# The last sequence's FC chunks led by four steps, and its last two chunks projected tile by tile

## The chip, the cores and the metric

The kernel runs on one core of one Trainium2 chip. The metric is the device time of one execution in microseconds; of several executions the median is taken. Beside the times there is one execution that the hardware profiler recorded; views of its trace are called "the profile" here. The engines of a core are TensorE (PE, its weight loads PEld), VectorE (DVE), ScalarE (ACT), GpSimd (POOL) and SyncE (SP), which issues the DMAs.

## The reference

The input is a batch of 8 sequences of 512 tokens by 512 features. A first stage adds to x a four-layer bidirectional gated recurrence (a linear scan) of the normalised x, fused by a matrix. The second stage, which the change is in, is a feed-forward block with ternary weights:

```python
h = jnp.einsum('btd,hd->bth', x, absmean(W_fc))       # 512 -> 2048
h = jax.nn.gelu(h, approximate=False)
h = layernorm(h, ln_w, ln_b)                          # over the 2048
return jnp.einsum('bth,dh->btd', h, absmean(W_proj))  # 2048 -> 512
```

Its input is the normalised result of the first stage, and its output is added to that result. absmean makes weights of -1, 0 and 1.

## The kernel before, in words

The recurrent stage takes lines 207 to 731 and leaves its result in DRAM. The feed-forward stage begins at line 739. Its order of work is written out by hand: the program issues instructions in the order of the code, and each engine runs its own in that order.

Names: B = 8 sequences, NF = 16 chunks of 128 hidden features, NT = 4 tiles of 128 tokens, NC_ = 4 chunks of 128 input features, LAG = 2.

- `fc(b, k)` (L777) computes chunk k of sequence b for all 512 tokens: eight matmuls (L782, four input chunks, each as a high and a low part) into one of two PSUM banks `ph`. ScalarE makes `g` (Gelu, L786), `sq` (L788) and `ghi` (L790, g times the norm's weight, rounded). VectorE adds g and sq to the running sums `acc` (L797), and makes the low part `glo` (L799).
- `proj(b, k, ghi, glo)` (L804) adds the chunk's share to the output: for each of the four token tiles two matmuls (L809) into that tile's own bank `po`, so eight matmuls. The four banks hold all 16 chunks' sums of a sequence.
- `token_stats(b)` (L814) makes the layer norm's mean and factor of each token from the two sums, which is possible only when all 16 chunks are in them: eight transposes on TensorE (L820), two reductions on VectorE (L821), small VectorE operations (L822 to L826), a power on GpSimd (L828). Its second half `last` (L830) makes `nmr` on VectorE (L832) and, for the last sequence only, the four centerings (L842) of the output rows.
- `finish(b)` (L849) empties the banks. For the last sequence VectorE does it, bank times the token's factor plus the row (L855), and `store` (L846) issues the tile's store on SP's queue. For the others ScalarE copies the banks (L859), and VectorE's centering and the store follow in later steps, one tile each, from the list `rests`.

The loop (L880) has a step j for each chunk of all sequences, and LAG more. In a step come, on TensorE: fc of chunk j, in the first step of a sequence the transposes of the statistics of the sequence before, and the projection of the chunk of two steps before. `waiting` holds the chunks between the two. Behind it come the second halves in `late`. The last sequence's chunks are j = 112 to 127. Steps 128 and 129 have no fc left: step 128 has the statistics' transposes, then the projection of chunk 126, then the rest of the statistics and the centerings; step 129 has the projection of chunk 127 and `finish`.

`gpool` holds g and sq three deep, `partp` holds ghi and glo four deep.

Of the kernel before, what the change touches and what calls it, by code (L numbers as in the profile page):

```python
# [9 lines left out]
F32 = mybir.dt.float32  # L10
F32R = mybir.dt.float32r
AF = mybir.ActivationFunctionType
ALU = mybir.AluOpType
# [3 lines left out]
P = 128  # L17
# [7 lines left out]
def kernel(  # L25
# [26 lines left out]
    nc = tc.nc  # L52
    B, S, H = x.shape
# [3 lines left out]
    NT = S // P  # L57
    NF = F // P
# [11 lines left out]
    tokp = ctx.enter_context(tc.tile_pool(name="tok", bufs=TOK))  # L70
# [21 lines left out]
    xs = {}  # L92
# [70 lines left out]
    def normalise(dst, src, rs_nmu, name):  # L163
        rs, nmu = rs_nmu
        nmr = small.tile([P, 1], F32, tag="nmr", name=f"nmr_{name}")
        nc.scalar.activation(nmr, nmu, AF.Copy, scale=rs)  # L166
        nc.scalar.activation(dst, src, AF.Identity, bias=nmr, scale=rs)  # L167
# [13 lines left out]
    def load_y(b):  # L181

        for t in range(NT):
            xs["y", b, t] = xsp.tile([P, H], F32, tag="xs", name=f"xy_{b}_{t}")
            nc.sync.dma_start(out=xs["y", b, t], in_=x1[b][t])
# [18 lines left out]
    rows = {}  # L204


    with rec:
# [129 lines left out]
        rx, scale = {}, {}  # L337
# [398 lines left out]

    gpool = ctx.enter_context(tc.tile_pool(name="g", bufs=3, reuse_waits="tile"))
    partp = ctx.enter_context(tc.tile_pool(name="parts", bufs=4, reuse_waits="tile"))  # L740
    accp = ctx.enter_context(tc.tile_pool(name="acc", bufs=1, reuse_waits="tile"))
    ps_x = ctx.enter_context(tc.tile_pool(name="ps_x", bufs=2, space=PSUM, reuse_waits="tile"))
    ps_o = ctx.enter_context(tc.tile_pool(name="ps_o", bufs=1, space=PSUM, reuse_waits="tile"))
    LAG = 2
# [30 lines left out]
    acc, po, first, stat = {}, {}, {}, {}  # L775

    def fc(b, k):  # L777
        ph = ps_f.tile([P, S], F32, tag="pf", name=f"ph_{b}_{k}")
        for c in range(NC_):
            w = fcq[k // NP_][:, c, ts(k % NP_, P)]  # L780
            for i in range(2):
                nc.tensor.matmul(  # L782
                    ph, lhsT=w, rhs=ys[b][c][i], start=(c == 0 and i == 0), stop=(c == NC_ - 1 and i == 1),
                )
        g = gpool.tile([P, S], F32, tag="g", name=f"g_{b}_{k}")
        nc.scalar.activation(g, ph, AF.Gelu)  # L786
        sq = gpool.tile([P, S], F32, tag="sq", name=f"sq_{b}_{k}")
        nc.scalar.activation(sq, g, AF.Square)  # L788
        ghi = partp.tile([P, S], F32R, tag="ghi", name=f"ghi_{b}_{k}")
        nc.scalar.activation(ghi, g, AF.Copy, scale=lnw[:, k : k + 1])  # L790
        if k == 0:
            first[b] = (g, sq)
        else:
            if k == 1:
                acc[b] = [accp.tile([P, S], F32, tag=f"acc{i}", name=f"acc{i}_{b}") for i in range(2)]
            for i, v in enumerate((g, sq)):
                nc.vector.tensor_tensor(acc[b][i], first[b][i] if k == 1 else acc[b][i], v, ALU.add)  # L797
        glo = partp.tile([P, S], F32R, tag="glo", name=f"glo_{b}_{k}")
        nc.vector.scalar_tensor_tensor(  # L799
            glo, g, lnw[:, k : k + 1], ghi.bitcast(F32), ALU.mult, ALU.subtract  # L800
        )
        return ghi, glo

    def proj(b, k, *parts):  # L804
        if k == 0:
            po[b] = [ps_o.tile([P, H], F32, tag=f"po{t}", name=f"po_{b}_{t}") for t in range(NT)]
        for t in range(NT):
            for i, part in enumerate(parts):
                nc.tensor.matmul(  # L809
                    po[b][t], lhsT=part[:, ts(t, P)], rhs=pwq[k // NP_][:, k % NP_, :],  # L810
                    start=(k == 0 and i == 0), stop=(k == NF - 1 and i == 1),
                )

    def token_stats(b):  # L814

        su = small.tile([P, 2, NT], F32, tag="su", name=f"su_{b}")
        for i, v in enumerate(acc.pop(b)):
            pst = ps_x.tile([P, 512], F32, tag="px", name=f"pst_{b}_{i}")
            for t in range(NT):
                nc.tensor.transpose(pst[:, ts(t, P)], v[:, ts(t, P)], ident)  # L820
            nc.vector.tensor_reduce(su[:, i, :], pst.rearrange("p (t f) -> p t f", t=NT), AX.X, ALU.add)  # L821
        nc.vector.tensor_scalar(su, su, 1.0 / F, None, ALU.mult)  # L822
        var = small.tile([P, NT], F32, tag="var", name=f"var_{b}")
        nc.vector.tensor_tensor(var, su[:, 0, :], su[:, 0, :], ALU.mult)
        nc.vector.tensor_tensor(var, su[:, 1, :], var, ALU.subtract)
        nc.vector.tensor_scalar(var, var, 0.0, LN_EPS, ALU.max, ALU.add)  # L826
        rs = small.tile([P, NT], F32, tag="rsg", name=f"rsg_{b}")
        nc.gpsimd.tensor_tensor(rs, var, mhalf.broadcast_to([P, NT]), ALU.pow)  # L828

        def last():  # L830
            nmr = small.tile([P, NT], F32, tag="nmrg", name=f"nmrg_{b}")
            nc.vector.scalar_tensor_tensor(nmr, su[:, 0, :], -1.0, rs, ALU.mult, ALU.mult)  # L832
            stat[b] = (rs, nmr)
            if b == B - 1:
                for t in range(NT):
                    center(b, t, xs["y", b, t])
        return last

    def center(b, t, rows_in):

        xt = xs["y", b, t]
        nc.vector.scalar_tensor_tensor(rows_in, rows[0], stat[b][1][:, t : t + 1], rows_in, ALU.mult, ALU.add)  # L842
        if rows_in is not xt:
            nc.vector.tensor_tensor(xt, xt, rows_in, ALU.add)

    def store(b, t):  # L846
        nc.sync.dma_start(out=out[b, ts(t, P), :], in_=xs["y", b, t])

    def finish(b):  # L849

        for t in range(NT):
            rs = stat[b][0][:, t : t + 1]
            if b == B - 1:
                row = xs["y", b, t]
                nc.vector.scalar_tensor_tensor(row, po[b][t], rs, row, ALU.mult, ALU.add)  # L855
                store(b, t)
            else:
                scaled = tokp.tile([P, H], F32, tag="tok", name=f"scaled_{b}_{t}")
                nc.scalar.activation(scaled, po[b][t], AF.Copy, scale=rs)  # L859

                def rest(t=t, scaled=scaled):
                    center(b, t, scaled)
                    store(b, t)
                rests.append(rest)

    rests = []
    found, ytok = {}, {}

    def y_stats(b, ts_):
        for t in ts_:  # L870
            found[t] = stats(xs["y", b, t], f"y{b}_{t}")

    def y_tokens(b, ts_):
        for t in ts_:
            tok = tokp.tile([P, H], F32, tag="tok", name=f"ytok_{b}_{t}")
            normalise(tok, xs["y", b, t], found.pop(t), f"y{b}_{t}")
            ytok.setdefault(b, []).append(tok)

    waiting = []
    for j in range(B * NF + LAG):  # L880
        b, k = divmod(j, NF)
        late = []
        if b < B:
            waiting.append((b, k, *fc(b, k)))
        if k == 0 and b > 0:
            late.append(token_stats(b - 1))
        if b == 0 and 5 <= k < 5 + NC_ + 3:
            row_piece(k - 5)
        if b + 1 < B and k >= NF - NC_:
            px = ps_x.tile([P, S], F32, tag="px", name=f"py_{b + 1}_{k}")  # L890
            late.append(y_chunk(b + 1, ytok[b + 1], k - (NF - NC_), px))
        if j >= LAG:
            done = waiting.pop(0)
            proj(*done)
        for f in late:
            f()
        if rests:
            rests.pop(0)()
        if j >= LAG and done[1] == NF - 1:
            finish(done[0])  # L900
        if b < B:
            at = 12 if b == 0 else 8
            if at <= k < at + NT:
                xt = xs["y", b, k - at]
                nc.vector.tensor_tensor(xt, xt, rows[1], ALU.add)
            if b + 1 < B:
                if k == 2:
                    load_y(b + 1)
                if k in (6, 7):
                    y_stats(b + 1, (2 * k - 12, 2 * k - 11))  # L910
                if k in (8, 9):
                    y_tokens(b + 1, (2 * k - 16, 2 * k - 15))


# [41 lines left out]
```

## Time and profile before

| | |
|---|---|
| median of 3 runs | 1767.56 us (1766.42 to 1767.7) |
| the profiled execution, its own time | 1769.31 us |
| its span, first to last instruction | 1767.3 us |
| mean granted TensorE clock | 0.990 |
| FC matmuls of the feed-forward stage (L782) | 1024 of 390 ns |
| projection matmuls (L809) | 512 of 398 ns, 512 of 390 ns |
| Gelu (L786) | 128 of 597 ns, idle before them 245.9 us, ended by PE ph |
| stores of the output | 32 of 256 KB, 2.0 us to landing |

A line of the timeline gives start, duration, engine, source line, operation, what it writes and reads, its shape and count, and in brackets the idle time before it and who ended it. A matmul's duration is longer than its distance to the next, since matmuls overlap; where a stage is bound by TensorE, the distance of the starts counts. Where several instructions are merged (x2, x4), the duration is from the first start to the last end.

### The profile page before, as it was taken

Reading aid. Unit: us, or ns where it says so; the run is one execution under the profiler, and the core shown is the slowest. Engines: PE = TensorE matmul, PEld = TensorE weight load, DVE = VectorE, ACT = ScalarE, POOL = GpSimd, SP = SyncE. Lnnn points to the kernel's source line nnn. Section 1 sums busy time; section 2 is a strip of 40 time slices with the busy share of each in tenths; the row PEclk is TensorE's granted clock in tenths of the full one; section 3 lists DMA queues with packets and bytes.
Section 4 is the critical chain, followed back from the end, with each engine's and each line's share of the span. In section 5 each row is a group of like instructions: output and inputs, shape, how many; then the busy total and the mean of one; then the engine's idle time right before and its main releaser. Section 6 shows DMA issues by size and latency. Waiting matters only on the chain.

```text
span 1767.3 us, 19729 instructions
## 1 busy us (share of the span) xinstructions
PE 1721.4 (97%) x6424; PEld 1046.7 (59%) x6424; DVE 1451.1 (82%) x2865; ACT 1066.2 (60%) x1836; POOL 214.5 (12%) x334
## 2 busy tenths in 40 slices
PE   7989999999999999999999999999999999999998
PEld 3554554455554445555444455554588888888886
DVE  6977989779999977999897799997468778778876
ACT  2887884358886325787632588872156556566653
POOL 1111111111111111111111111111000000000000
PEclk9999999999999999999999999999999999999999
DMA  7002210110231111123101201101301101101100
GB/s 262 12 30 78 96 54 19 48 48 13 72 102 54 28 38 54 36 72 107 49 24 42 96 13 48 59 14 42 126 1 48 38 11 48 49 9 40 48 24 24
DMA packets 46454, 91.73 MB, mean 52 GB/s; under 512 B 5264, under 2 KB 5264, under 8 KB 45328
## 3 DMA queue, kind: packets, MB, share of 16 engines
q1 hardware_dynamic: 45488, 88.91, 14.8%
q10 hardware_dynamic: 864, 1.57, 0.3%
q8 instruction: 50, 0.82, 0.2%
q14 instruction: 52, 0.43, 0.1%
HBM read 65.30 MB, written 25.17 MB: 51 GB/s over the span
## 4 chain that ended last, share of the span: by engine, by line
PE 62%; DVE 29%; issue 6%; ACT 2%; POOL 0%; DVEq 0%; DMA 0%; POOLq 0%; ACTq 0%
PE u L414 16%; PE pu L528 12%; PE ph L782 12%; PE po L809 11%; DVE z L442 7%; DVE st L149 5%; DVE z L438 4%; PE u L457 4%; PE pt L293 3%; DVE z L497 2%; PE pf L302 2%; DVE a L437 2%; DVE mv L151 1%; DVE ve L155 1%; DVE st_x L149 1%
## 5 line engine op out<-in xcount | busy, mean ns | idle before, releaser
L414 PE MATMUL u<-xT,gw 128*128 128x512 f32 x768 | 351.1, 601 | 0.0
L414 PE MATMUL u<-h,gw 128*128 128x512 f32 x768 | 350.7, 600 | 0.0
L442 DVE TENSOR_TENSOR_SCAN z<-a,z 128x512 f32<-128x512 f32 x224 | 274.3, 1224 | 7.8
L149 DVE BATCH_NORM_STATS2 st<-pt 128x6 f32<-128x512 f32 x256 | 177.2, 692 | 71.7 <-PE pt L293 71.2
L786 ACT ACTIVATE g<-ph 128x512 f32<-128x512 f32 x128 | 76.4, 597 | 245.9 <-PE ph L782 245.9
L414 PEld LDWEIGHTS u<-xT,gw 128*128 128x128 f32 x768 | 141.2, 194 | 141.0 <-issue 141.0
L414 PEld LDWEIGHTS u<-h,gw 128*128 128x128 f32 x768 | 141.1, 194 | 140.7 <-issue 140.7
L156 POOL TENSOR_TENSOR rs<-ve,mhalf 128x1 f32<-128x1 f32 x192 | 122.9, 640 | 704.1 <-DVE nmu L160 649.1
L809 PE MATMUL po<-pwq,ghi 128*128 128x512 f32 x512 | 203.6, 398 | 0.0
L809 PE MATMUL po<-pwq,glo 128*128 128x512 f32 x512 | 199.9, 390 | 0.0
L782 PE MATMUL ph<-yhi,fcq 128*128 128x512 f32 x512 | 199.8, 390 | 0.0
L782 PE MATMUL ph<-ylo,fcq 128*128 128x512 f32 x512 | 199.7, 390 | 0.0
L431 ACT ACTIVATE a<-u,ngb 128x512 f32<-128x512 f32 x192 | 131.2, 683 | 99.6 <-PE u L414 98.7
L438 DVE TENSOR_TENSOR z<-z,t 128x512 f32<-128x512 f32 x224 | 153.7, 686 | 16.6 <-ACT z L433 16.6
L167 ACT ACTIVATE tok<-pt,nmr,rs 128x512 f32<-128x512 f32 x192 | 149.2, 777 | 6.4
L797 DVE TENSOR_TENSOR acc<-acc,g 128x512 f32<-128x512 f32 x112 | 77.4, 691 | 91.1 <-ACT g L786 90.1
L433 ACT ACTIVATE z<-u,gb 128x512 f32<-128x512 f32 x192 | 132.6, 691 | 0.0
L431 ACT ACTIVATE a<-z,ngb 128x512 f32<-128x512 f32 x32 | 23.1, 722 | 179.7 <-DVE z L464 179.7
L432 ACT ACTIVATE t<-u,gb 128x512 f32<-128x512 f32 x192 | 131.0, 682 | 0.0
L302 PE MATMUL pf<-ident,tok 128*128 128x128 f32 x768 | 116.8, 276 | 13.0 <-ACT tok L167 10.4
L293 PEld LDWEIGHTS pt<-ident,z 128*128 128x128 f32 x640 | 78.8, 142 | 84.6 <-issue 52.4
L166 ACT ACTIVATE nmr<-nmu,rs 128x1 f32<-128x1 f32 x192 | 56.5, 294 | 107.5 <-POOL rs L156 96.8
(138 smaller groups left out, 2711.0 us busy)
## 6 DMA issues: line engine op xcount, KB each, us to landing
xn<-in_x_dram SPq DMA_DIRECT2D x32, 256.0 KB, 4.6
xf<-in_x_dram SPq DMA_DIRECT2D x32, 256.0 KB, 4.3
x<-xf SPq DMA_DIRECT2D x32, 256.0 KB, 2.0
xy<-x SPq DMA_DIRECT2D x32, 256.0 KB, 4.1
out_dram<-xy SPq DMA_DIRECT2D x32, 256.0 KB, 2.0
xT<-in_xt_dram SPq DMA_DIRECT2D x7, 1024.0 KB, 7.0
fca<-in_fc_wT_dram SPq DMA_DIRECT2D x16, 256.0 KB, 2.9
pwa<-in_proj_wT_dram SPq DMA_DIRECT2D x16, 256.0 KB, 2.7
```

The costliest lines, as they stand in the source:

```text
L149: nc.vector.bn_stats(st, src)
L167: nc.scalar.activation(dst, src, AF.Identity, bias=nmr, scale=rs)
L293: nc.tensor.transpose(pt[:, ts(c, P)], zs[c][:, ts(t, P)], ident)
L302: nc.tensor.transpose(pf[:, ts(t, P)], toks[t][:, ts(c, P)], ident)
L414: nc.tensor.matmul(u, lhsT=gw[l][:, c, ts(o, P)], rhs=h[:, c, :], start=(c == 0), stop=(c == NC_ - 1),)
L431: nc.scalar.activation(a, u, AF.Sigmoid, bias=ngb[:, l, o : o + 1], scale=-1.0)
L433: nc.scalar.activation(z, u, AF.Sigmoid, bias=gb[:, l, o : o + 1])
L438: nc.vector.tensor_tensor(z, z, t, ALU.mult)
L442: nc.vector.tensor_tensor_scan(dst[:, d], a[:, d], z[:, d], 0.0, ALU.mult, ALU.add)
L528: nc.tensor.matmul(pu, lhsT=hs[d][:, c, ts(t, P)], rhs=fw[:, d * NC_ + c, :], start=(c == 0), stop=(c == NC_ - 1),)
L782: nc.tensor.matmul(ph, lhsT=w, rhs=ys[b][c][i], start=(c == 0 and i == 0), stop=(c == NC_ - 1 and i == 1),)
L809: nc.tensor.matmul(po[b][t], lhsT=part[:, ts(t, P)], rhs=pwq[k // NP_][:, k % NP_, :], start=(k == 0 and i == 0), stop=(k == NF - 1 and i ...
```

## The change

The loop now has as many steps as there are chunks (128). In steps 124 and 125 two FC chunks are issued rather than one, so that steps 126 and 127 have none left, and up to five chunks wait for their projection; `partp` is five deep for that. The statistics of the last sequence come in step 126, ahead of the projection of chunk 124. After the loop chunks 126 and 127 are left: for each token tile the two matmuls of chunk 126 and the two of chunk 127 are issued, and right behind them that tile's bank is emptied and stored. The computation itself is the same.

```diff
-    partp = ctx.enter_context(tc.tile_pool(name="parts", bufs=4, reuse_waits="tile"))
+    partp = ctx.enter_context(tc.tile_pool(name="parts", bufs=5, reuse_waits="tile"))
...
-    def proj(b, k, *parts):
+    def proj(b, k, *parts, tiles=range(NT)):
...
-        for t in range(NT):
+        for t in tiles:
             for i, part in enumerate(parts):
                 nc.tensor.matmul(
...
         for t in range(NT):
             rs = stat[b][0][:, t : t + 1]
-            if b == B - 1:
-                row = xs["y", b, t]
-                nc.vector.scalar_tensor_tensor(row, po[b][t], rs, row, ALU.mult, ALU.add)
+            scaled = tokp.tile([P, H], F32, tag="tok", name=f"scaled_{b}_{t}")
+            nc.scalar.activation(scaled, po[b][t], AF.Copy, scale=rs)
+
+            def rest(t=t, scaled=scaled):
+                center(b, t, scaled)
                 store(b, t)
-            else:
-                scaled = tokp.tile([P, H], F32, tag="tok", name=f"scaled_{b}_{t}")
-                nc.scalar.activation(scaled, po[b][t], AF.Copy, scale=rs)
-
-                def rest(t=t, scaled=scaled):
-                    center(b, t, scaled)
-                    store(b, t)
-                rests.append(rest)
+            rests.append(rest)
+
+    def finish_last(b, t):
+        row = xs["y", b, t]
+        nc.vector.scalar_tensor_tensor(row, po[b][t], stat[b][0][:, t : t + 1], row, ALU.mult, ALU.add)
+        store(b, t)
...
-    for j in range(B * NF + LAG):
+    ends = B * NF
+    todo = [(b, k) for b in range(B) for k in range(NF)]
+    for j in range(ends):
         b, k = divmod(j, NF)
         late = []
-        if b < B:
-            waiting.append((b, k, *fc(b, k)))
+        for _ in range(2 if ends - 4 <= j < ends - 2 else 1):
+            if todo:
+                waiting.append((*todo[0], *fc(*todo[0])))
+                todo.pop(0)
+        if j == ends - 2:
+            late.append(token_stats(b))
         if k == 0 and b > 0:
             late.append(token_stats(b - 1))
...
+    for t in range(NT):
+        for done in waiting:
+            proj(*done, tiles=(t,))
+        finish_last(B - 1, t)
```

The lines left out at the end take away one level of indentation where `if b < B` is now always true.

More of the change, by code (lines that the diff above doesn't have):

```diff
@@ L900 @@
             finish(done[0])
[L901 to L912, printed above, removed]
+        at = 12 if b == 0 else 8
+        if at <= k < at + NT:
+            xt = xs["y", b, k - at]
+            nc.vector.tensor_tensor(xt, xt, rows[1], ALU.add)
+        if b + 1 < B:
+            if k == 2:
+                load_y(b + 1)
+            if k in (6, 7):
+                y_stats(b + 1, (2 * k - 12, 2 * k - 11))
+            if k in (8, 9):
+                y_tokens(b + 1, (2 * k - 16, 2 * k - 15))
+    for t in range(NT):
+        for done in waiting:
+            proj(*done, tiles=(t,))
+        finish_last(B - 1, t)
 def kernel(**inputs):
```

## The prediction

> **What bounds the kernel now.** I read the page's busy rows first, then the change's own stretch (the last sequence, from 1740 us on) as windows, and then the timeline of single engines in it.
>
> ```profile
> PE 1721.4 (97%) x6424; PEld 1046.7 (59%) x6424; DVE 1451.1 (82%) x2865; ACT 1066.2 (60%) x1836; POOL 214.5 (12%) x334
> ```
>
> TensorE carries the span as a whole, and the change takes no matmul away. So only TensorE's gaps and what follows its last matmul can be won. The windows show where that is:
>
> ```profile
> 1740.00:1752.60 12.60, 12.60 (x57) 10.46 (x56) 7.71 (x12) 5.77 (x10) 0.00 (x0) 1.00 0.00 1
> ...
> 1755.40:1759.30 3.90, 3.88 (x19) 2.88 (x16) 2.60 (x9) 0.00 (x0) 1.01 (x1) 1.00 0.00 0
> 1759.30:1761.00 1.70, 0.00 (x0) 0.00 (x0) 1.70 (x4) 0.00 (x0) 0.00 (x0) 1.00 0.00 0
> 1761.00:1763.00 2.00, 0.00 (x0) 0.00 (x0) 2.00 (x4) 0.00 (x0) 0.00 (x0) 0.78 0.00 0
> ```
>
> Columns: stretch, then busy PE, PEld, DVE, ACT, POOL, and the granted clock. TensorE is full until 1759.3 us. Then it is done, and VectorE (third figure) works alone. What it works on, in the timeline of VectorE:
>
> ```profile
> 1754.77 0.75 DVE L799 SCALAR_TENSOR_TENSOR glo<-g,lnw,ghi 128x512 fp32r<-128x512 f32 x1
> 1755.44 1.28 DVE L821 TENSOR_REDUCE su<-pst 128x4 f32<-128x512 f32 x2
> ...
> 1758.65 0.16 DVE L832 SCALAR_TENSOR_TENSOR nmrg<-su,rsg 128x4 f32<-128x4 f32 x1 [1.13 <-POOL rsg L828]
> 1758.85 2.74 DVE L842 SCALAR_TENSOR_TENSOR xy<-row,nmrg,xy 128x512 f32<-128x512 f32 x4
> 1761.51 2.72 DVE L855 SCALAR_TENSOR_TENSOR xy<-po,rsg,xy 128x512 f32<-128x512 f32 x4
> ```
>
> The reader is to see one unbroken chain: glo of chunk 127, two reductions, the small statistics, 1.13 us waiting for GpSimd's power, four centerings (L842), four evictions (L855). From the start of the reductions (1755.44) to the end of the last eviction (1761.51 + 2.72 = 1764.23) it takes 8.79 us. All four banks were complete at 1758.89 + 0.39 = 1759.28, before the first eviction starts. So the end is set by the token statistics coming late, not by the banks. After 1764.23 come the last store and the closing (1767.3 - 1764.23 = 3.1 us), which the change leaves as they are.
>
> **The change part by part.** Pitches from the timeline: eight matmuls take 1.81 us (an FC chunk's first at 1750.85, the next projection's at 1752.66), a step of both 3.63 us.
>
> *Two FC chunks a step at 124 and 125.* No instruction is added; FC chunks move ahead of projections on TensorE. Old order of the end: fc 127 (from 1750.85), proj 125, statistics' transposes (from 1754.48), proj 126, proj 127. New order from step 124's start (1739.97): fc 124, fc 125, proj 122 (to 1745.41); fc 126, fc 127, proj 123 (to 1750.85); transposes; proj 124, 125, then 126 and 127 by tiles. The transposes thus start 1754.48 - 1750.85 = 3.63 us earlier, if the sums are there. When are they? fc 127 ends at 1749.03 instead of 1752.66. ScalarE and VectorE now get chunks every 1.81 us instead of every 3.63. The trace of before has that very case where the stage is filled, three FC chunks in a row from 1268.9 us:
>
> ```profile
> 1272.53 0.60 ACT L786 ACTIVATE g<-ph 128x512 f32<-128x512 f32 x1
> 1273.16 0.63 ACT L788 ACTIVATE sq<-g 128x512 f32<-128x512 f32 x1
> 1273.70 0.71 ACT L790 ACTIVATE ghi<-g,lnw 128x512 fp32r<-128x512 f32 x1
> 1274.34 0.60 ACT L786 ACTIVATE g<-ph 128x512 f32<-128x512 f32 x1
> ```
> ```profile
> 1274.49 0.75 DVE L799 SCALAR_TENSOR_TENSOR glo<-g,lnw,ghi 128x512 fp32r<-128x512 f32 x1
> 1275.15 0.69 DVE L797 TENSOR_TENSOR acc<-acc,g 128x512 f32<-128x512 f32 x1
> 1275.75 0.69 DVE L797 TENSOR_TENSOR acc<-acc,sq 128x512 f32<-128x512 f32 x1
> 1276.35 0.75 DVE L799 SCALAR_TENSOR_TENSOR glo<-g,lnw,ghi 128x512 fp32r<-128x512 f32 x1
> ```
>
> ScalarE keeps the pace (1274.34 - 1272.53 = 1.81). VectorE needs 1276.35 - 1274.49 = 1.86 a chunk, hardly more. On the new clock: Gelu starts 0.42 after its last matmul starts (1752.44 to 1752.86). So Gelu 126 starts at 1747.42, its ghi 1.17 later at 1748.59, done 1749.30; glo 126 starts at 1749.33. Glo 127 follows 1.86 later, at 1751.19, and the reductions 0.67 after it (1754.77 to 1755.44): 1751.86. That is 1755.44 - 1751.86 = 3.58 us earlier. The first sum is complete at 1749.33 + 0.66 + 0.69 = 1750.68, before TensorE asks at 1750.85; the second at 1751.28, when the first four transposes (0.9 us for eight) end. TensorE so waits 0 to 0.1 us. The other bound for VectorE: 1.95 a chunk, its pitch where it waits for each operand (1753.49, 1754.16, 1754.77, 1755.44); the shift is then 3.49. I take 1.86, the row with the same queueing.
>
> *Statistics at step 126.* The same 8 transposes, 7 VectorE operations, power and 4 centerings, moved past two projections. Queued behind the transposes on TensorE are now four projections (124 to 127), 32 matmuls of 0.226 = 7.25 us, where there were two. A late sum holds all of them. Behind the power's 1.13 us wait on VectorE stand only centerings and evictions, as before.
>
> *Tile by tile.* The same 16 matmuls in another order, each with its own weights as before. TensorE's total is the same, so its last matmul still starts near 1758.9 and po3 is complete at 1759.3; a tile is four matmuls, 0.91 us, so the banks are complete at 1756.57, 1757.48, 1758.38, 1759.29. VectorE reaches its evictions at 1761.51 - 3.58 = 1757.93 and then every 0.66: 1757.93, 1758.59, 1759.25, 1759.91. Each bank has been complete for 1.36, 1.11, 0.87 and 0.62 us. So this part is worth nothing: VectorE never waits for a bank, and chunk-by-chunk order would do as well. Its cover is those 0.62 us: TensorE may be 0.6 us late before it shows.
>
> *Stores.* Four on SP's queue, behind their evictions at the same 0.66 spacing; they move as a block. No other DMA runs there. Price 0.
>
> *Fifth buffer.* With the lead, chunk 127 takes the buffer of chunk 122, whose projection ends at 1745.41, five us before ghi 127 is written. It moves later tiles' addresses; nothing in the trace shows a cost of place (L782 and L809 read operands of different pools at 390 ns alike). Bound: 0 to 10 ns a step over 128 steps, so up to 1.3 us, and no reason for a gain. I take 0. Buffers of g and of ph are kept three and two deep; the three chunks in a row at the start show no stall in that.
>
> *Clock, by trace and by rule.* The new wait of TensorE at the transposes could cost clock. The trace: last matmul ends at 1759.28, and the window 1761 to 1763 has a mean of 0.78, which is a halving at about 1762.1, 2.8 us later. The Trainium skill (TensorE: Matmul & The Clock Gate, "What's actually happening") puts the fall to half rate after an idle window of some 3.4 us. By the row a wait of 2.8 us, by the rule one of 3.4 us, would slow the 32 matmuls behind it by 7.2 us. At my 0.1 us both give 0.
>
> Sum: 0 for all parts but the moved statistics, -3.58. Profiled span 1767.3 to 1763.7; its own time 1769.31 to 1765.7. That execution is 1.75 us above the median shown; on the median: 1767.56 - 3.58 = 1764.0.
>
> **The rivals.** *Main case*: VectorE's chain still sets the end, 3.3 to 3.8 us earlier, 1763.8 to 1764.3. Chance 0.78.
>
> *A, late sums.* The two chunks queue up on VectorE and ScalarE worse than at the stage's start (there acc had no history, and no wait for g). For it: slack before the first transposes is only 0.17 us. Against: the 1.86 row. A chain late by 0.5 to 2.5 us gains 1.1 to 3.1: 1764.5 to 1766.5. Chance 0.10.
>
> *B, TensorE's banks become the end*, and the tile order does work. Needs a statistics chain shorter by over 0.62 us, for which no row speaks. The last eviction would start at 1759.33 rather than 1763.49: gain 4.15, 1763.4. Chance 0.08.
>
> *C, slower: the clock falls at the transposes.* Place: TensorE waiting for acc with four projections behind it. Price: 2.8 us of wait plus 7.2 us of half clock, po3 complete at 1769.3, evicted at 1770.1 against 1764.23: 5.8 slower, 1773.4. It decides once po3 is complete after 1763.49, 4.2 us late. Against it: granted clock 1.00 in every window up to 1761, and a wait of 0.1. Chance 0.04.
>
> That the tile order does not do what it says is part of the main case.
>
> **How the numbers follow.** The runs shown scatter by 1.3 us, so the main case spreads over about 1762.8 to 1765.2; with half of A and most of B the range 1762.8 to 1765.8 holds 0.8. What a measurement of this kernel can tell from no change is about 0.2%, 3.54 us. My forecast lies on that bound: just over half of the main case is beyond it. Faster: 0.41 + B 0.08 = 0.49. Within: 0.37 + A 0.10 = 0.47. Slower: C, 0.04.
>
> **What the profile after would show.** Right: reductions from about 1751.9, no DVE idle before an eviction, last eviction ending near 1760.7, PE ending near 1759.3. A: PE idle before the transposes, DVE acc starts late. B: evictions at a 0.91 pitch with idle put down to PE po. C: clock under 1.00 before 1761. I am wrong if another wait appears in steps 124 to 127, or if steps before 124 are not 3.63 as now.

## The result and the profile after

The changed kernel takes 1764.65 us (median of 15 runs, 1762.86 to 1766.1), the kernel before, in 15 runs, 1767.79 (1766.15 to 1769.35). The ratio is 0.9981, with a 95% interval of 0.9973 to 0.9988. That is 3.14 us faster. The interval leaves "no change" out, but the gain is a little under the 0.2% (3.54 us) on which the forecast lay: 1764.0, a gain of 3.58 us.

Total times scatter by some 3 us within each kernel, so the work is better read inside the profile. The page's first line after, against the one shown of before:

```profile
PE 1720.1 (98%) x6424; PEld 1045.1 (59%) x6424; DVE 1450.8 (82%) x2865; ACT 1066.1 (60%) x1836; POOL 214.4 (12%) x334
```

The same number of instructions on each engine, in a span of 1762.6 us rather than 1767.3. Not all of the 4.7 us belongs to the change: the stage's first FC matmul starts at 1267.11 us here and at 1268.26 before, and the code ahead of it is the same. I therefore compare **stage lengths**: from that first matmul to the end of the last eviction. The first matmul, before and after:

```profile
1268.26 0.79 PE L782 MATMUL ph<-yhi,fcq 128*128 128x512 f32 x1
```
```profile
1267.11 0.79 PE L784 MATMUL ph<-yhi,fcq 128*128 128x512 f32 x1
```

Before: 1764.23 - 1268.26 = 495.97. After, from VectorE's timeline of the end (the changed kernel's lines have higher numbers: L799 is L801 here, L821 L823, L842 L844 and L855 L865):

```profile
1750.05 0.74 DVE L801 SCALAR_TENSOR_TENSOR glo<-g,lnw,ghi 128x512 fp32r<-128x512 f32 x1
1750.71 1.28 DVE L823 TENSOR_REDUCE su<-pst 128x4 f32<-128x512 f32 x2
...
1753.93 0.16 DVE L834 SCALAR_TENSOR_TENSOR nmrg<-su,rsg 128x4 f32<-128x4 f32 x1 [1.13 <-POOL rsg L830]
1754.12 2.74 DVE L844 SCALAR_TENSOR_TENSOR xy<-row,nmrg,xy 128x512 f32<-128x512 f32 x4
1756.78 2.72 DVE L865 SCALAR_TENSOR_TENSOR xy<-po,rsg,xy 128x512 f32<-128x512 f32 x4
```

1756.78 + 2.72 - 1267.11 = 492.39, which is 3.58 less. The reader is to see that it is the same chain as before, link for link: reductions to end of last eviction 8.79 us, and still no bracket with an idle time in front of the evictions. It only starts earlier. The windows of the end say the same from TensorE's side:

```profile
1738.80:1758.20 19.40, 19.40 (x89) 15.57 (x87) 15.57 (x29) 7.54 (x13) 1.01 (x1) 1.00 0.00 0
1758.20:1759.50 1.30, 0.00 (x0) 0.00 (x0) 1.30 (x2) 0.00 (x0) 0.00 (x0) 1.00 0.86 321
```

VectorE alone now works for 1.3 us behind TensorE's last matmul, where it was 1764.23 - 1759.28 = 4.95 before. From the end of the last eviction to the end of the span are 3.1 us in both kernels.

### The profile page after: what moved, and what is told of

Same layout as the page of the kernel before. It is cut to its first block, busy times and chain, and to the rows that moved or that the text cites. A ratio compares the mean times of both kernels' runs of the same rounds, so it can differ in the third digit from the quotient of the medians.

```text
span 1762.6 us, 19721 instructions
## 1 busy us (share of the span) xinstructions
PE 1720.1 (98%) x6424; PEld 1045.1 (59%) x6424; DVE 1450.8 (82%) x2865; ACT 1066.1 (60%) x1836; POOL 214.4 (12%) x334
## 4 chain that ended last, share of the span: by engine, by line
PE 61%; DVE 29%; issue 6%; ACT 3%; POOL 0%; DMA 0%; DVEq 0%; POOLq 0%; ACTq 0%
PE u L414 16%; PE ph L784 12%; PE po L811 11%; PE pu L528 11%; DVE z L442 7%; DVE st L149 5%; DVE z L438 4%; PE u L457 4%; PE pt L293 3%; DVE z L497 2%; PE pf L302 2%; DVE a L437 2%; DVE mv L151 1%; DVE ve L155 1%; DVE st_x L149 1%
## 5 line engine op out<-in xcount | busy, mean ns | idle before, releaser
L799 DVE TENSOR_TENSOR acc<-acc,g 128x512 f32<-128x512 f32 x112 | 77.3, 691 | 87.8 <-ACT g L788 86.9
L302 PE MATMUL pf<-ident,tok 128*128 128x128 f32 x768 | 116.2, 275 | 13.0 <-ACT tok L167 10.4
```

What stands on the lines that cost most here:

```text
L302: nc.tensor.transpose(pf[:, ts(t, P)], toks[t][:, ts(c, P)], ident)
```

## The experiments

Each edit is shown against the changed kernel, unless said. Nine kernels, one profile each; e1, e2 and e3 also have medians, which stand beside 1767.41 us of the kernel before (41 other runs than the 15 above).

**e1, the lead without the tile order.**

```diff
-    for t in range(NT):
-        for done in waiting:
-            proj(*done, tiles=(t,))
-        finish_last(B - 1, t)
+    for done in waiting:
+        proj(*done)
+    for t in range(NT):
+        finish_last(B - 1, t)
```

> The FC lead and the early statistics as changed, but the last two chunks projected chunk by chunk and the four banks emptied afterwards. Measure: stage length, from the first FC matmul of the feed-forward stage to the end of the last eviction (before 495.97 us, after 492.39). Theory: the statistics' chain on VectorE sets the end and every bank is complete before VectorE reaches it, so 492.4, and a time within 0.1 us of the changed kernel. Rival (the tile order gives part of the gain): 492.8 to 494.

Measured: 1764.81 us, ratio 0.9983 (0.9976 to 0.999). Stage length, from the first FC matmul at 1265.99:

```profile
1753.01 2.74 DVE L844 SCALAR_TENSOR_TENSOR xy<-row,nmrg,xy 128x512 f32<-128x512 f32 x4
1755.76 2.73 DVE L865 SCALAR_TENSOR_TENSOR xy<-po,rsg,xy 128x512 f32<-128x512 f32 x4
```

1758.49 - 1265.99 = 492.50. The evictions start 2.75 behind the centerings instead of 2.66: they wait 0.09 us for the first bank, whose last matmul starts at 1755.33. So the lead with its early statistics gives 3.47 of the 3.58 us, and the tile order 0.11. (No run has the lead without the early statistics.)

**e2, the tile order without the lead** (edit against the changed kernel: the lead and its early statistics are taken back).

```diff
-        for _ in range(2 if ends - 4 <= j < ends - 2 else 1):
+        for _ in range(1):
...
-        if j == ends - 2:
-            late.append(token_stats(b))
...
+    token_stats(B - 1)()
     for t in range(NT):
         for done in waiting:
```

> The tile order alone: no FC lead, statistics where they were before (ahead of chunk 126), the last two chunks projected tile by tile, each bank emptied and stored behind its matmuls. Theory: no gain, stage length 496.0, time as before. Rival (tile order gives the gain): 492.5 to 495.5.

Measured: 1768.15 us, ratio 1.0002 (0.9994 to 1.001). Its first FC matmul starts at 1266.76, its evictions are

```profile
1760.01 2.72 DVE L865 SCALAR_TENSOR_TENSOR xy<-po,rsg,xy 128x512 f32<-128x512 f32 x4
```

1762.73 - 1266.76 = 495.97, to the hundredth that of before. Alone the tile order does nothing, and neither does the fifth buffer, which this kernel keeps.

**e3, three double steps.** The parts of chunk 127 are put in buffers that the stage's input has left (the two lines for that are left out here).

```diff
-        for _ in range(2 if ends - 4 <= j < ends - 2 else 1):
+        for _ in range(2 if ends - 6 <= j < ends - 3 else 1):
...
-        if j == ends - 2:
+        if j == ends - 3:
```

> Three double FC steps (122 to 124), statistics one step earlier (125), tile order kept; the parts of chunk 127 lie in freed buffers of the stage's input. Theory: VectorE reaches its evictions 1.81 us earlier, so the banks now set the end: last bank complete as in the changed kernel, evictions about 0.91 apart with idle put down to TensorE, stage length 491.9, 0.5 shorter than the changed kernel. If the chain of VectorE were still the end: 490.6. If the longer run of FC chunks queues up: over 492.4.

Measured: 1763.73 us (13 runs), ratio 0.9979 (0.9971 to 0.9987). VectorE's end:

```profile
1753.04 2.74 DVE L844 SCALAR_TENSOR_TENSOR xy<-row,nmrg,xy 128x512 f32<-128x512 f32 x4
1756.24 0.75 DVE L865 SCALAR_TENSOR_TENSOR xy<-po,rsg,xy 128x512 f32<-128x512 f32 x1 [0.47 <-PE po L811]
1757.15 0.75 DVE L865 SCALAR_TENSOR_TENSOR xy<-po,rsg,xy 128x512 f32<-128x512 f32 x1 [0.15 <-PE po L811]
1758.05 0.75 DVE L865 SCALAR_TENSOR_TENSOR xy<-po,rsg,xy 128x512 f32<-128x512 f32 x1 [0.16 <-PE po L811]
1758.96 0.75 DVE L865 SCALAR_TENSOR_TENSOR xy<-po,rsg,xy 128x512 f32<-128x512 f32 x1 [0.15 <-PE po L811]
```

This is what banks that set the end look like: four evictions 0.91 apart, each with an idle time put down to TensorE's po. Stage length 1759.71 - 1267.83 = 491.88. Of the 1.81 us by which the statistics came earlier only 0.51 is left; then TensorE's last matmul is the end. In the time its gain over the changed kernel lies within the scatter.

**e4, e3 with chunk order** (e1's edit on e3).

> As e3, but the last two chunks projected chunk by chunk. Theory: the first bank is complete 1.36 us before the last, and four evictions of 0.66 behind it end at 492.5: the tile order is worth 0.6 us here, though it is worth nothing in e1. If the tile order is never worth anything: as e3, 491.9.

Measured, in one run, 1764.08 us; first FC matmul at 1266.51:

```profile
1756.28 2.73 DVE L865 SCALAR_TENSOR_TENSOR xy<-po,rsg,xy 128x512 f32<-128x512 f32 x4 [1.82 <-PE po L811]
```

Stage length 1759.01 - 1266.51 = 492.50. The evictions wait 1.82 us for the first bank and then follow at VectorE's own pace. Tile order is worth 492.50 - 491.88 = 0.62 us once the statistics are out of the way.

**e5, no centerings** (the four centerings of the last sequence are left out).

```diff
-            if b == B - 1:
-                for t in range(NT):
-                    center(b, t, xs["y", b, t])
```

> The changed kernel without the four centerings of the last sequence (that part of its output lacks the mean's term). Theory: VectorE's chain is 2.66 us shorter, but the banks then set the end: stage length 491.9, 0.5 less than the changed kernel. Rival (the chain alone sets the end, no second bound near): 489.7.

Measured, the first and the last eviction (L862 here):

```profile
1756.56 0.75 DVE L862 SCALAR_TENSOR_TENSOR xy<-po,rsg,xy 128x512 f32<-128x512 f32 x1 [1.43 <-PE po L811]
...
1759.28 0.75 DVE L862 SCALAR_TENSOR_TENSOR xy<-po,rsg,xy 128x512 f32<-128x512 f32 x1 [0.15 <-PE po L811]
```

Stage length 1760.03 - 1268.15 = 491.88, the same as e3 by another way, with the same pattern of evictions. So 2.66 us less work on VectorE's chain brings 0.51.

**e6 and e7, TensorE made later.** Two, then six matmuls more ahead of the last two chunks (e6's edit; e7 has 6 and 5 for 2 and 1).

```diff
+    spare = ps_x.tile([P, H], F32, tag="px", name="spare")
+    for i in range(2):
+        nc.tensor.matmul(spare, lhsT=waiting[0][2][:, ts(0, P)], rhs=pwq[3][:, 2, :], start=(i == 0), stop=(i == 1))
     for t in range(NT):
```

> The changed kernel with two more matmuls (into a bank that nothing reads) ahead of the last two chunks: TensorE 0.45 us later. Theory: the cover is about 0.5 us (last bank complete at 1758.20, last eviction from 1758.76), so 492.4, no change. Rival (the banks set the end): 492.85.

> As e6 with six more matmuls: TensorE 1.36 us later, 0.85 beyond the cover. Theory: 493.2. Rival (the banks set the end): 493.75. Rival (VectorE has much more cover than 0.5): 492.4.

Measured: stage length of e6 1757.97 - 1265.61 = 492.36, of e7 1759.21 - 1266.00 = 493.21. TensorE's last matmul and the last eviction of e7:

```profile
1758.03 0.39 PE L811 MATMUL po<-pwq,glo 128*128 128x512 f32 x1
1758.46 0.75 DVE L865 SCALAR_TENSOR_TENSOR xy<-po,rsg,xy 128x512 f32<-128x512 f32 x1 [0.15 <-PE po L811]
```

Counted from the first FC matmul, TensorE's last matmul starts at 490.70 in the changed kernel (1757.81 - 1267.11), at 491.12 in e6 (1756.73 - 1265.61) and at 492.03 in e7. So TensorE is 0.42 us later in e6, which costs nothing, and 1.33 later in e7, which costs 0.82. The cover, the time that TensorE may be late before it shows, is 1.33 - 0.82 = 0.51 us: the same as the gain at which e3 and e5 stop.

**e8 and e9, sums made late.** Glo of chunk 126 is made four times (e8), seven times (e9), which holds VectorE ahead of the sums of chunk 127 (e8's edit, indentation left aside; e9 has 7 for 4).

```diff
+        for _ in range(4 if (b, k) == (B - 1, NF - 2) else 1):
             nc.vector.scalar_tensor_tensor(
                 glo, g, lnw[:, k : k + 1], ghi.bitcast(F32), ALU.mult, ALU.subtract
             )
```

> The changed kernel with glo of chunk 126 made four times instead of once, which puts the sums of chunk 127 2.0 us later. Theory: the whole chain moves with it, stage length 494.4; TensorE waits about 1.85 us at the transposes, and its granted clock stays at 1.00 as that is under the 2.8 us after which it fell in the trace of before. If late sums were absorbed: 492.4.

Measured, TensorE's transposes and VectorE's evictions:

```profile
1752.29 1.23 PE L823 MATMUL pst<-ident,acc 128*128 128x128 f32 x8 [2.19 <-DVE acc L799]
```
```profile
1759.39 2.72 DVE L866 SCALAR_TENSOR_TENSOR xy<-po,rsg,xy 128x512 f32<-128x512 f32 x4
```

The reductions start at 1753.32, that is 485.95 behind the first FC matmul (1267.37), where the changed kernel has 483.60; stage length 1762.11 - 1267.37 = 494.74. So the chain moves as a whole, by 2.35; the three repeats took more than the 0.67 each that I had put down. TensorE waits 2.19 us at the transposes at a clock of 1.00.

> The changed kernel with glo of chunk 126 made seven times, sums 4.0 us later. By the clock's row in the trace of before (fall 2.8 us after the last matmul)[...] TensorE's wait of 3.85 us halves its clock, and 32 matmuls behind it take 7.2 us more: the banks set the end, stage length about 502.9. If a wait of that length leaves the clock alone: 496.4, VectorE's chain moved by 4.0.

Measured: stage length 1764.91 - 1266.87 = 498.04, between the two values expected. TensorE's timeline shows the wait and what follows:

```profile
1754.17 1.94 PE L823 MATMUL pst<-ident,acc 128*128 128x128 f32 x8 [4.55 <-DVE acc L799]
1755.77 0.78 PE L812 MATMUL po<-pwq,ghi 128*128 128x512 f32 x1
...
1757.19 0.58 PE L812 MATMUL po<-pwq,glo 128*128 128x512 f32 x1
1757.61 0.40 PE L812 MATMUL po<-pwq,ghi 128*128 128x512 f32 x1
```

And its windows, with the granted clock as the third figure from the end:

```profile
1749.60:1754.00 4.40, 0.03 (x1) 0.00 (x0) 4.26 (x7) 0.12 (x1) 0.00 (x0) 1.00 0.00 0
1754.00:1757.60 3.60, 3.42 (x12) 3.09 (x13) 3.29 (x9) 0.00 (x0) 0.00 (x0) 0.53 0.00 0
1757.60:1764.00 6.40, 6.40 (x29) 5.07 (x27) 5.08 (x9) 0.00 (x0) 1.01 (x1) 1.00 0.12 43
```

The clock does fall, but only at the end of the wait, and it is back after some 3.4 us (the mean of 0.53 over 3.6 us is 3.4 us at half). Eight transposes and four projection matmuls run slow, not 32: from the first transpose to the last matmul's start are 1763.74 - 1754.17 = 9.57 us, against 1757.81 - 1749.70 = 8.11 in the changed kernel, so TensorE lost 1.46 us. VectorE's first reduction and its last eviction:

```profile
1755.30 0.69 DVE L824 TENSOR_REDUCE su<-pst 128x4 f32<-128x512 f32 x1
...
1764.16 0.75 DVE L866 SCALAR_TENSOR_TENSOR xy<-po,rsg,xy 128x512 f32<-128x512 f32 x1 [0.15 <-PE po L812]
```

The stage is 498.04 - 492.39 = 5.65 us longer than the changed kernel's. The late sums account for 4.83 of it: the reductions start 1755.30 - 1266.87 = 488.43 behind the first FC matmul, where the changed kernel has 483.60. TensorE's slow stretch adds the other 0.82: the second reduction, which waits for the transposes, comes 0.26 us late, and the last two evictions, which wait for po (0.16 and 0.15 us idle), add 0.56.

## Why the prediction was right, and where it was not

**The moved statistics: right, to the hundredth in the stage.** The step took VectorE's pitch of 1.86 us a chunk from the stage's start (its three FC chunks begin at 1268.26, not at 1268.9 as the step says; the pitch is not touched by that). In the changed kernel, glo of chunk 126 and of chunk 127:

```profile
1748.18 0.75 DVE L801 SCALAR_TENSOR_TENSOR glo<-g,lnw,ghi 128x512 fp32r<-128x512 f32 x1
1748.85 0.69 DVE L799 TENSOR_TENSOR acc<-acc,g 128x512 f32<-128x512 f32 x1
1749.45 0.69 DVE L799 TENSOR_TENSOR acc<-acc,sq 128x512 f32<-128x512 f32 x1
1750.05 0.74 DVE L801 SCALAR_TENSOR_TENSOR glo<-g,lnw,ghi 128x512 fp32r<-128x512 f32 x1
```

1750.05 - 1748.18 = 1.87. The other bound, 1.95, would have been wrong: here no line from the one to the other has a wait in brackets, so the operands are ready when VectorE comes to them. Counted from the first matmul of FC chunk 124 (1739.97 before, 1738.82 after), the reductions start at 15.47 and 11.89, which is 3.58 earlier. Rival A, late sums, did not come about; e8 shows what it would have cost, since a delay of the sums goes one to one into the end.

**TensorE's wait: right.** Expected were 0 to 0.1 us. Counted from FC chunk 124's start, its last matmul starts at 18.99, where before it was 18.92, so at most 0.07 was lost.

**The tile order: right that it is next to nothing, not quite nothing.** I had said that chunk order would do as well; e1 makes that 0.11 us, since in chunk order the first bank is complete only as VectorE arrives. The step gave the banks' times for the tile order alone. The cover of 0.62 us was 0.51 (e6, e7). Both differences of 0.11 have the same two parts: TensorE was 0.07 later, and an eviction starts 0.43 after its bank's last matmul starts (1758.53 to 1758.96 in e3), where I had counted 0.39.

**Rival B was the next bound, as placed:** take the statistics (e3) or the centerings (e5) out of the way and the banks set the end, at 495.97 - 491.88 = 4.09 us under before, where 4.15 was worked out. It needed a chain shorter by another 0.51 us, and no part of the change brought that.

**Rival C: the mechanism exists, its price was wrong.** The step let the half clock last for all 32 matmuls, 7.2 us. In e9 it lasted about 3.4 us, cost TensorE 1.46 and moved the end by 0.82. By an estimate from this, one such spell costs TensorE at most half of 3.4, that is 1.7 us, and the cover takes up to 0.51 of it, so it could have eaten a part of the 3.58 us and not turned the gain round. That e9's stage is 2.1 us longer than before comes from its late sums. The condition was wrong too: neither 2.8 nor 3.4 us of wait is where the clock falls in these traces (last section).

**Fifth buffer, stores, closing: right at 0.** The end behind the last eviction is 3.1 us in both, and e2, with five buffers, is as long as before. From the first FC matmul to FC chunk 124's are 471.71 us in both kernels (1739.97 - 1268.26 and 1738.82 - 1267.11).

**From stage to time.** The times moved by 3.14 us where the stage moved by 3.58; the ratio's interval spans 2.1 to 4.8 us and holds both, and the two sets of runs of the kernel before have medians 0.38 us apart (1767.79 and 1767.41). The prediction had put the scatter at 1.3 us, from three runs; with 15 it is 3.2. It gave 0.49 to a gain beyond 0.2% and 0.47 to one within, so a gain just within decides nothing between the two. In the eleven profiles scatter comes from ahead of the change: the first FC matmul starts anywhere from 1265.61 to 1268.26 us, with the same code before it. The granted clock differs there from execution to execution: over 550 to 600 us its mean is 0.98 in before and 0.94 in after (lines of this stretch stand in the last section). That stretch alone does not settle the start of the stage: e7 has 0.97 there and starts it at 1266.00, e5 has 0.95 and starts it at 1268.15. A part of the scatter is there from the first work on: the program's first eight matmuls (L655) take 6.70 us in before's profile, 6.30 in after's, 5.38 in e6's and 5.30 in e7's, and these four start the stage at 1268.26, 1267.11, 1265.61 and 1266.00. That the clock makes the whole of the scatter no experiment here has shown.

## What to carry to other kernels

At the end of a kernel, find which chain is still running when TensorE has stopped, and ask whether its start can be moved rather than its last link: here the statistics' lead was worth 3.5 us, and handing over the banks one by one 0.1. Then work out the next bound: the lead could be lengthened for 0.5 us more, and only then does the order by tiles pay (0.6 us). For a change of a few microseconds, compare distances inside the profile between two events that enclose it; here they repeated to a few hundredths of a microsecond (495.97 twice, 491.88 twice, 492.39 and 492.36) where the times scattered by three.

## What the runs showed of the hardware

- The length of TensorE's wait alone did not decide whether its granted clock fell. Behind its last matmul the clock fell 2.8 us on in before (from the windows in the prediction) and 3.0 us on in the changed kernel, whose window 1761.00 to 1762.60 has a mean of 0.55. In e9 it held for nearly all of a wait of 4.55 us, and in e8 through one of 2.19. Far ahead of the change both kernels have the same wait at L302. First before's wait and the window behind it, then after's:

```profile
551.32 0.33 PE L302 MATMUL pf<-ident,tok 128*128 128x128 f32 x1 [2.40 <-ACT tok L167]
552.00:556.00 4.00, 4.00 (x14) 2.03 (x14) 3.00 (x5) 2.58 (x5) 0.00 (x0) 1.00 0.00 0
```
```profile
548.38 0.33 PE L302 MATMUL pf<-ident,tok 128*128 128x128 f32 x1 [2.39 <-ACT tok L167]
549.50:552.70 3.20, 3.20 (x5) 1.25 (x4) 2.56 (x4) 1.70 (x3) 0.00 (x0) 0.50 0.00 0
```

In before the clock stays at 1.00, from 548.30 on. In after it is at half, from about a microsecond after work had resumed. So a wait of 2.4 us can be followed by a fall or not, and that e8's wait of 2.19 us left the clock at 1.00 does not make 2.19 us safe. What decides it no run here separates.

- The spell at half clock behind a wait lasted about 3.4 us in e9 and in after: there the 0.2 us ahead of the window shown have a mean of 0.79 and the 0.8 us behind it one of 0.92, so 0.08 + 3.20 + 0.13 = 3.4.
- Repeats of one VectorE operation on the same output had a longer pitch than different ones in a row: seven glo in 5.48 us (e9), so (5.48 - 0.75) / 6 = 0.79 each, against 0.66 from a glo to the next operation on another tile, and (2.74 - 0.75) / 3 = 0.66 for the four centerings, one operation on four outputs. Whether the engine or a wait of the program's own between two writes of one tile makes the difference no run shows.
